# Ordering on VectorE around a deformable convolution: the combining step and the depthwise taps

## The chip, the core and the metric

The kernel runs on one core of a Trainium2 chip. The metric is device time in microseconds (us) of one execution; lower is better. TensorE is PE in the profile, VectorE is DVE, ScalarE is ACT, GpSimd is POOL, and SP only issues DMAs.

## What is computed

The input is 32 images of 96 channels, 56 x 56 pixels, in float32. Two layers follow each other.

Layer 0 is an inverted residual block: a 1x1 convolution from 96 to 576 channels with SiLU, a 3x3 depthwise convolution with SiLU, a squeeze-and-excite gate, and a 1x1 convolution back to 96 channels, added to the input.

```python
h = silu(bn(conv1x1(x, w1)))
h = silu(bn(depthwise3x3(h, w2)))
h = h * se_gate(mean(h))
x1 = x + bn(conv1x1(h, w3))
```

Layer 1 makes an attention map from a Fourier magnitude, and then mixes an ordinary 3x3 convolution with a deformable one, whose nine taps are sampled bilinearly at learned offsets:

```python
y = x1 * ca * sa
offset = conv3x3(aux(y), off_w)
gate = sigmoid(conv1x1(relu(conv3x3(aux(y), dg1_w)), dg2_w))
y_def = einsum(bilinear_samples(y, offset), def_w) + def_b
z = (1 - gate) * conv3x3(y, base_w) + gate * y_def
out = relu(batchnorm(z) + x1)
```

## The kernel before

**Tiling.** Layer 1 goes through an image in seven bands of 8 rows (`j` from 0 to 6), and each band in two halves (`h`) of 28 columns. The main loop runs over all 224 bands (32 images by 7). While it works on image b, two generators ("streams") are advanced step by step inside it: `second(b + 1)` (projection of layer 0, Fourier part, attention) and `first(b + 2)` (expansion and depthwise convolution of layer 0). The function `pump()` advances them in proportion to the slots passed, and also runs functions that were put into the list `later` with a due slot.

**Who sets the order.** The Python code traces the instructions in one order. A scheduler then orders each engine's queue: by trace order as priority, and by its own model of when an instruction's inputs are ready. SP's queue alone is kept in traced order. A queue, once built, is executed strictly in its order, and each instruction waits there for its semaphores. Some instructions are pinned (`keep_in_program_order`): the product of the column and row weights (L710) is one of them, so it comes behind what was traced ahead of it on DVE.

**What a half band does** (L1136 and the lines behind it). `sample_tiles` (L739) multiplies transposed blocks of y by the bilinear weights `wc`, in two groups of matmuls; ScalarE copies the samples to `v` (L743) and packs them (L750). `deform` (L758) multiplies `v` by the deformable weights into the PSUM tile `pd`. That call is put into `ends` and made in the next half band, behind the first group of `sample_tiles`. Then, in the same place, come the blocks for a coming half (L721, L725, L727) and the product `wc = wc * wr` on DVE (L710) for the next half band's samples. So DVE's product of weights is always traced behind `ends`.

**The pool of `pd`** has one buffer. Both halves of a band write to one `pd`; `combine` (L797 to L800) reads it on DVE in its first instruction, and the first product of the next band may start only when that first instruction has ended. Before the change `end_half` puts `join`, which calls `combine`, into `later`, due two slots on.

**The offsets.** `offsets` runs a joint 3x3 convolution (L615) for the band two ahead of the main loop, ScalarE takes two parts out of its PSUM bank (L635, L637), and DVE copies the offsets out in two copies, `at` (L664). The bank comes free behind these copies. GpSimd then sends `at` to memory (L672).

**The taps.** The depthwise convolution is done by DVE: for each of nine units per image one multiplication (L260) and eight multiply-adds over 128 x 1512 or 128 x 1568 elements (L262). The first two images use matmuls for three of the taps (L246, L258). When a unit is complete, ScalarE applies SiLU (L222).

**Others on DVE** that matter here: the sums over the spectrum `m_fe` and `m_fy` (L436, L437), which PE waits for in L440; the sums of squares (L379); the largest offset, `top` (L676).

Of the kernel before, what the change touches and what calls it, by code (L numbers as in the profile page):

```python
# [1 line left out]

# [8 lines left out]
ALU = mybir.AluOpType  # L11
# [5 lines left out]
C, H, W = 96, 56, 56  # L17
# [18 lines left out]
BW = NBW  # L36
TS = 4
NTX = W // TS
# [79 lines left out]
def bank(p):  # L118
    return p["mm"].tile([128, 512], FP, name="mm")
# [84 lines left out]
def hidden(tc, p, x, xn, h2d, pooled, defer):  # L204


    nc = tc.nc
    w = p["w0"]

    def rows_of(x, half):  # L210
        xt = p["xt"].tile([C, (HH + 1) * W], FP, name="xt")
        r0 = half * (HH - 1)
        nc.sync.dma_start(xt, x[:, r0 : r0 + HH + 1].rearrange("c h w -> c (h w)"))
        return xt

    xts = p.pop("xts", None) or [rows_of(x, 0), rows_of(x, 1)]
    for _ in expand(nc, p, xts, UNITS[0]):
        yield
    def finish(u, acc):
        ch = UNITS[u][0]  # L220
        flat = acc.rearrange("p h w -> p (h w)")
        tc.keep_in_program_order(nc.scalar.activation(  # L222
            flat, flat, AF.Silu, bias=w["sh2"][:, ch : ch + 1], scale=w["inv2"][:, ch : ch + 1], accum_out=pooled[:, u : u + 1]))
        nc.scalar.dma_start(h2d[u], flat)

    before = None
    for u, (ch, half) in enumerate(UNITS):
        h1 = p["h1"]
        more = expand(nc, p, xts, UNITS[u + 1]) if u + 1 < len(UNITS) else iter(())
        if xn is not None and u in (5, 8):  # L230

            p.setdefault("xts", []).append(rows_of(xn, int(u == 8)))
        acc = p["acch"].tile([128, HH, W], FP, name="acch")

        rows_of_tap = lambda dy: (int(half == 0 and dy == 0), HH - int(half == 1 and dy == 2))
        diag = p.get("diag")
        taps = [k for k in (4, 0, 1, 2, 3, 5, 6, 7, 8) if diag is None or k not in TPE]
        parts = []
        if diag is not None:
            for r0 in range(0, HH, ER):  # L240
                pt = bank(p)[:, :EW].rearrange("p (h w) -> p h w", h=ER)
                for i, k in enumerate(TPE):
                    dy, dx = divmod(k, 3)
                    lo, hi = rows_of_tap(dy)
                    lo, hi = max(r0, lo), min(r0 + ER, hi)
                    nc.tensor.matmul(pt[:, lo - r0 : hi - r0], diag[:, ch, i], h1[:, dy + lo : dy + hi, dx : dx + W],  # L246
                                     start=(i == 0), stop=(i == len(TPE) - 1))
                parts.append((slice(r0, r0 + ER), pt))
            next(more, None)
            yield  # L250
        for n, k in enumerate(taps):
            dy, dx = divmod(k, 3)
            lo, hi = rows_of_tap(dy)
            win = h1[:, dy + lo : dy + hi, dx : dx + W]
            wk = w["w2"][:, ch, k : k + 1]
            if n == 0:
                for rs, pt in parts:
                    nc.vector.scalar_tensor_tensor(acc[:, rs], win[:, rs], wk, pt, ALU.mult, ALU.add)  # L258
                if not parts:
                    nc.vector.tensor_scalar(acc, win, wk, None, ALU.mult)  # L260
            else:
                nc.vector.scalar_tensor_tensor(acc[:, lo:hi], win, wk, acc[:, lo:hi], ALU.mult, ALU.add)  # L262
            if n % 2:
                if n == 3 and before:
                    finish(u - 1, before)
                next(more, None)
                yield
        for _ in more:
            pass
        before = acc  # L270
    defer(lambda: finish(len(UNITS) - 1, before))


def sigmoid(nc, out, src, bias):
# [354 lines left out]
def joint_conv(nc, p, yp, j, hid):  # L629


    w = p["w"]
    pa = bank(p)
    conv3(nc, pa[:, :BW], w["joint"], yp, CJ, j)
    nc.scalar.activation(hid, pa[:DMID, :BW], AF.Relu, bias=w["dg1b"][:DMID])  # L635
    yb = p["yb"].tile([C, BW], FP, name="yb")
    nc.scalar.activation(yb[BC:], pa[OFF0 + QC :, :BW], AF.Identity, bias=w["cv"]("base_b")[BC:])  # L637
    yield yb, pa[OFF0 : OFF0 + NOFF, :BW]
    pb = bank(p)
    for k in range(NTAP):  # L640
        dy, dx = divmod(k, 3)
        r0 = j * RB + dy + PD - 1
        for i in range(2):
            nc.tensor.matmul(pb[i * BC : (i + 1) * BC, : BW // 2].rearrange("p (h w) -> p h w", h=RB // 2), w["base"][:, k],  # L644
                             yp[:C, r0 + i * RB // 2 : r0 + (i + 1) * RB // 2, dx + PD - 1 : dx + PD - 1 + W],
                             start=(k == 0), stop=(k == NTAP - 1))
    yield
    for i in range(2):
        nc.scalar.activation(yb[:BC, i * BW // 2 : (i + 1) * BW // 2], pb[i * BC : (i + 1) * BC, : BW // 2], AF.Identity,
                             bias=w["cv"]("base_b")[:BC])  # L650
    yield


def offsets(nc, p, yp, j, top, hid, ybs, hds, defer):

    w = p["w"]
    joint = joint_conv(nc, p, yp, j, hid)
    yb, pa = next(joint)  # L660
    ybs.append(yb)
    at = p["off"].tile([NOFF, NTX, 2, TP], FP, name="at")
    for s in range(2):
        nc.vector.tensor_copy(at[:, :, s].rearrange("o t (r c) -> o t r c", r=TS),  # L664
                              pa[:, s * BW // 2 : (s + 1) * BW // 2].rearrange("o (r t c) -> o t r c", r=TS, t=NTX))
    yield
    yield
    next(joint)
    yield
    od = p["dp"].tile([NTX, 2, NOFF, TP], FP, name="od")  # L670
    p["tc"].keep_in_program_order(
        nc.gpsimd.dma_start(od.rearrange("t s o p -> o (t s) p"), at.rearrange("o t s p -> o (t s) p")))  # L672
    next(joint)
    yield
    next(joint, None)
    nc.vector.tensor_reduce(top, at.rearrange("o t s p -> o (t s p)"), AX.X, ALU.max, apply_absolute_value=True)  # L676
    for _ in range(7):
        yield
    ht = p["ht"].tile([SB * NTX, 4, KP], FP, name="ht")
    src = od.rearrange("t s o p -> t (s o p)").unsqueeze(0).to_broadcast([SB, NTX, 4 * KP])  # L680
    nc.sync.dma_start(ht.rearrange("q n k -> q (n k)"), src)
    for _ in range(3):
        yield

    def hats():
        ho = p["ht"].tile([SB * NTX, 2, 2, KP], FP, name="ho")
        p["tc"].keep_in_program_order(nc.scalar.activation(
            ho.rearrange("q x s n -> q s x n"), ht.rearrange("q (s x) n -> q s x n", s=2), AF.Abs, bias=w["blk"]))
        nc.scalar.activation(ho, ho, AF.Relu, bias=w["one"], scale=-1.0)
        hd = p["dp"].tile([2, 2, SB, NTX, KP], FP, name="hd")  # L690
        nc.scalar.dma_start(hd.rearrange("x s i t n -> (i t) (x s) n"), ho.rearrange("q x s n -> q (x s) n"))
        hds.append(hd)

    defer(hats)
# [99 lines left out]
def combine(nc, p, j, pd, yb, gate, st):  # L794

    z = p["q2"].tile([C, BW], FP, name="z")
    nc.vector.scalar_tensor_tensor(z, pd[:C, :BW], p["w"]["cv"]("def_b"), yb, ALU.add, ALU.subtract)  # L797
    nc.vector.scalar_tensor_tensor(z, gate, 1.0, z, ALU.add, ALU.mult)
    nc.vector.scalar_tensor_tensor(z, z, 0.5, yb, ALU.mult, ALU.add)
    nc.vector.bn_stats(st[:, j], z)  # L800
    return z
# [152 lines left out]
def layers(tc, a, dp, x1d, zd, stats, far):  # L954
# [6 lines left out]
    nc = tc.nc  # L961
    B = x1d.shape[0]
    with ExitStack() as ctx:
        p = {"tc": tc, "dp": ctx.enter_context(tc.tile_pool(name="l1d", bufs=3, space=DRAM))}
# [25 lines left out]
        streams, later = [], []  # L990
        slot = 0
# [68 lines left out]
        def store(b, j, z):  # L1060
            nc.gpsimd.dma_start(zd[b][:, j * BW : (j + 1) * BW], z)

        def join(n, pd, gate, st):
            b, j = bands[n]
            z = combine(nc, p, j, pd, ybs[n], gate, st)
            later.append((slot + 7, lambda: store(b, j, z)))
            if j == NBD - 1:
                nc.vector.bn_aggr(stats[:, b], st)

        def end_half(n, h, v, gate, st):  # L1070
            if h == 0:
                pds[n] = p["pd"].tile([128, 512], FP, name="pd")
            deform(nc, p, pds[n], v, h)
            if h:
                pd = pds.pop(n)
                later.append((slot + 2, lambda: join(n, pd, gate, st)))

        ends, pds = [], {}

# [41 lines left out]
        for n, (b, j) in enumerate(bands):  # L1121
            if j == 0:
                st = p["st"].tile([C, NBD, 6], FP, name="st")
# [7 lines left out]
            for h in range(2):  # L1131
                v = p["vp"].tile([128, NTAP, NTH, 2, TP], FP, name="v")
                prepare(2 * n + h + READY + AHEAD)
                s = ready.pop(0)
# [17 lines left out]
                if h == 0:  # L1152
                    if n % 2 == 0:
                        gates.extend(gates_of(nc, p, hids[n // 2]))
                    gate = gates.pop(0)
# [361 lines left out]
```

## Time and profile before

| what | value |
|---|---|
| median of 3 runs | 9030.57 us (9027.98 to 9034.88) |
| the profiled execution: its time / the span of its instructions | 9059.03 us / 9057.2 us |
| mean granted TensorE clock | 0.939 |
| PE busy | 8175.3 us, 90% of the span |
| DVE busy | 7184.4 us, 79% |
| ACT busy | 5393.5 us, 60% |
| POOL busy | 2902.8 us, 32% |
| the 2250 plain taps, L262 on DVE | 4456.4 us, 1981 ns each |

How to read it: busy time is the time in which an engine has an instruction at work. A line `engine line <- releaser: us, times, longest` in the table of waits is idle time of the first engine that ended when the second one finished. In the timeline each row is one instruction, or several of one kind that follow each other: start, duration, engine, line, operation, `output<-inputs`, and in brackets the idle time before it and what ended it. Durations of one row overlap those of the next by some tens of ns; on PE by more, as matmuls are pipelined.

### The profile page before, as it was taken

To read this page: it belongs to the slowest core of one execution; us is meant where nothing else is said; L and a number is where in the kernel's file an instruction comes from. 1 tells how busy PE (TensorE), PEld (TensorE's weight loads), DVE (VectorE), ACT (ScalarE), POOL (GpSimd) and SP (SyncE) were. 2 spreads that over 40 slices of the span, in tenths; PEclk is the share of its full clock that TensorE was granted. 3 is DMA by queue.
4 is the path that set the end of the run, shared out by engine and by line. 5 is a ranking of instruction groups with operands and counts; after the bars stand their busy time and mean duration, and the time that the engine had idled before them with its cause. 6 is when DMAs were issued, how large, how long until landed. Compare 5 with 4: busy or idle time off the path is not lost. (4 is left out here: it accounts for less than half of the span.)

```text
span 9057.2 us, 137476 instructions
## 1 busy us (share of the span) xinstructions
PE 8175.3 (90%) x52406; PEld 5193.5 (57%) x52406; DVE 7184.4 (79%) x6629; ACT 5393.5 (60%) x10486; POOL 2902.8 (32%) x2800
## 2 busy tenths in 40 slices
PE   5889999999999999999999999999999999999960
PEld 3456565665656566565656656565665655566640
DVE  7688888888888888888888888888888888888333
ACT  2356665666666666666666666666666666666553
POOL 0233333333333333333333333333333333333210
PEclk9889999999999999999999999999999999999985
DMA  2356666666666666666666666666666666666669
GB/s 82 108 142 160 163 169 165 157 154 153 163 166 171 166 157 147 158 165 164 172 161 154 159 157 168 165 174 161 154 154 160 165 166 172 166 156 144 144 188 416
DMA packets 1068758, 1486.48 MB, mean 164 GB/s; under 512 B 590191, under 2 KB 839839, under 8 KB 1055807
## 3 DMA queue, kind: packets, MB, share of 16 engines
q1 hardware_dynamic: 858995, 985.20, 46.4%
q10 hardware_dynamic: 153803, 329.80, 10.2%
q0 software_dynamic: 55296, 162.60, 6.7%
q8 instruction: 420, 6.88, 0.4%
q14 instruction: 244, 1.99, 0.1%
HBM read 1064.29 MB, written 412.65 MB: 163 GB/s over the span
## 5 line engine op out<-in xcount | busy, mean ns | idle before, releaser
L262 DVE SCALAR_TENSOR_TENSOR acch<-hp,w,acch 128x1512 f32<-128x1512 f32 (+1 forms) x2250 | 4456.4, 1981 | 141.4 <-ACT hp L173 103.8
L615 PE MATMUL mm<-yp,c_jointW 104*128 104x448 f32 x4032 | 1679.6, 568 | 10.1 <-DMA yp<-fqd 10.1
L758 PE MATMUL pd<-v,c_def 128*96 128x224 f32 (+1 forms) x6272 | 1468.8, 382 | 142.7 <-DVE z L797 115.6
L721 POOL COPY ybl<-yp 96x448 f32<-96x448 f32 x896 | 1048.3, 1198 | 1204.9 <-PE mm L725 1204.8
L758 PEld LDWEIGHTS pd<-v,c_def 128*96 128x96 f32 (+1 forms) x6272 | 1062.2, 176 | 449.8 <-issue 116.9
L615 PEld LDWEIGHTS mm<-yp,c_jointW 104*128 104x128 f32 x4032 | 776.6, 196 | 784.2 <-issue 747.4
L743 ACT COPY v<-mm 96x288 f32<-96x288 f32 (+1 forms) x2688 | 1004.3, 441 | 156.0 <-PE mm L739 109.3
L169 PE MATMUL mm<-xt,w 96*128 96x392 f32 (+3 forms) x2688 | 1058.5, 527 | 35.3 <-DMA xt<-in_x 33.1
L739 PE MATMUL mm<-wc,yt 64*96 64x144 f32 x12544 | 1056.9, 300 | 20.8 <-DVE sq L379 6.7
L739 PEld LDWEIGHTS mm<-wc,yt 64*96 64x96 f32 x12544 | 834.2, 164 | 317.3 <-issue 199.1
L173 ACT ACTIVATE hp<-mm,sh,inv 128x392 f32<-128x392 f32 (+2 forms) x1216 | 810.7, 673 | 344.8 <-PE mm L169 290.5
L710 DVE TENSOR_TENSOR wc<-wc,wr 128x1008 f32<-128x1008 f32 x448 | 566.6, 1265 | 412.5 <-DMA wr<-hd 385.1
L644 PE MATMUL mm<-yp,c_base0W 96*64 96x224 f32 x8064 | 830.1, 358 | 5.7 <-ACT hp L173 5.7
L329 PE MATMUL mm<-hq,w3s 128*96 128x392 f32 x2048 | 749.7, 510 | 63.6 <-DMA hq<-h2d 62.2
L672 POOL DMA_DIRECT2D od<-at x224 | 186.7, 834 | 1908.3 <-DVE at L664 1292.6
L750 ACT COPY v<-v 32x448 f32<-32x448 f32 x1344 | 755.1, 562 | 29.7
L727 ACT COPY yt<-mm 128x384 f32<-128x384 f32 (+1 forms) x896 | 353.9, 439 | 700.7 <-PE mm L725 699.0
L644 PEld LDWEIGHTS mm<-yp,c_base0W 96*64 96x64 f32 x8064 | 555.2, 135 | 282.7 <-issue 61.0
L635 ACT ACTIVATE hid<-mm,c_dg1b 50x448 f32<-50x448 f32 x224 | 140.8, 628 | 868.4 <-PE mm L615 858.4
L476 POOL TENSOR_TENSOR o<-o,xc 96x392 f32<-96x392 f32 x256 | 376.2, 1470 | 806.2 <-ACT o L339 804.2
L222 ACT ACTIVATE acch<-acch,sh,inv 128x1568 f32<-128x1568 f32 x288 | 488.4, 1696 | 202.8 <-DVE acch L262 176.5
L329 PEld LDWEIGHTS mm<-hq,w3s 128*96 128x96 f32 x2048 | 323.0, 166 | 395.2 <-issue 367.5
(194 smaller groups left out, 9325.3 us busy)
## 6 DMA issues: line engine op xcount, KB each, us to landing
h2d<-acch ACTq DMA_DIRECT2D x288, 784.0 KB
wc<-hd SPq DMA_DIRECT2D x896, 252.0 KB
wr<-hd SPq DMA_DIRECT2D x448, 504.0 KB
hq<-h2d SPq DMA_DIRECT2D x128, 980.0 KB
hq<-h2d SPq DMA_DIRECT2D x128, 784.0 KB
hq<-x1d SPq DMA_DIRECT2D x768, 98.0 KB
ht<-od SPq DMA_DIRECT2D x224, 252.0 KB
hd<-ho ACTq DMA_DIRECT2D x224, 252.0 KB
```

Source lines behind the costliest of these rows:

```text
L169: nc.tensor.matmul(pt[p0 : p0 + w1.shape[1], : rows * W], w1, xts[hf][:, r0 * W : (r0 + rows) * W], start=True, stop=True)
L173: nc.scalar.activation(h1[lo:hi, row0 : row0 + rows, 1 : 1 + W], pt[lo:hi, : rows * W].rearrange("p (h w) -> p h w", h=rows), AF.Silu, bia ...
L262: nc.vector.scalar_tensor_tensor(acc[:, lo:hi], win, wk, acc[:, lo:hi], ALU.mult, ALU.add)
L329: nc.tensor.matmul(pts[half][:C, :EW], w3s[:, ch], hq, start=(i == 0), stop=False)
L615: nc.tensor.matmul(view, weights[:, k], yp[:channels, r0 : r0 + RB, dx + PD - 1 : dx + PD - 1 + W], start=(k == 0), stop=(k == NTAP - 1))
L644: nc.tensor.matmul(pb[i * BC : (i + 1) * BC, : BW // 2].rearrange("p (h w) -> p h w", h=RB // 2), w["base"][:, k], yp[:C, r0 + i * RB // 2 ...
L710: p["tc"].keep_in_program_order(nc.vector.tensor_tensor(wc, wc, wr, ALU.mult))
L721: nc.gpsimd.tensor_copy(yb[:, :, s], blocks)
L739: nc.tensor.matmul(pt[k][:C, (t - lo) * KP : (t - lo + 1) * KP], yt[ps, t], s[ps, t * KP : (t + 1) * KP], start=True, stop=True)
L743: nc.scalar.copy(v[:C, :, lo:hi, k].rearrange("c k t p -> c t k p"), pt[k][:C, : (hi - lo) * KP].rearrange("c (t k p) -> c t k p", t=hi - ...
L750: nc.scalar.copy(v[C:, 1 + 2 * i : 3 + 2 * i], v[i * QC : (i + 1) * QC, KA:])
L758: nc.tensor.matmul(out.rearrange("c q (t x) -> c t q x", x=TS), p["w"]["def"][ks, k], v[ks, k].rearrange("c t s (r x) -> c t (s r) x", r=T ...
```

## The change

Three edits, all of them about order. No instruction is added or removed, and no size changes.

1. `join`, and so `combine`, is called at once behind the second half's products, in place of two slots later.
2. The first instruction of `combine` and each of the two copies of the offsets is remembered in `p["urgent"]`.
3. Each tap traced on DVE afterwards (L258, L262; not the first multiplication, L260) gets an edge behind the instruction that `urgent` names at that time. The edge has no semaphore: it only tells the scheduler that the tap must stand behind it in DVE's queue.

```diff
             if n == 0:
-                for rs, pt in parts:
-                    nc.vector.scalar_tensor_tensor(acc[:, rs], win[:, rs], wk, pt, ALU.mult, ALU.add)
+                with behind(p):
+                    for rs, pt in parts:
+                        nc.vector.scalar_tensor_tensor(acc[:, rs], win[:, rs], wk, pt, ALU.mult, ALU.add)
                 if not parts:
                     nc.vector.tensor_scalar(acc, win, wk, None, ALU.mult)
             else:
-                nc.vector.scalar_tensor_tensor(acc[:, lo:hi], win, wk, acc[:, lo:hi], ALU.mult, ALU.add)
+                with behind(p):
+                    nc.vector.scalar_tensor_tensor(acc[:, lo:hi], win, wk, acc[:, lo:hi], ALU.mult, ALU.add)
...
+def behind(p):
+
+    return p["tc"].issue_after(p["urgent"]) if "urgent" in p else nullcontext()
...
     for s in range(2):
-        nc.vector.tensor_copy(at[:, :, s].rearrange("o t (r c) -> o t r c", r=TS),
-                              pa[:, s * BW // 2 : (s + 1) * BW // 2].rearrange("o (r t c) -> o t r c", r=TS, t=NTX))
+        p["urgent"] = nc.vector.tensor_copy(
+            at[:, :, s].rearrange("o t (r c) -> o t r c", r=TS),
+            pa[:, s * BW // 2 : (s + 1) * BW // 2].rearrange("o (r t c) -> o t r c", r=TS, t=NTX)).ins
...
-    nc.vector.scalar_tensor_tensor(z, pd[:C, :BW], p["w"]["cv"]("def_b"), yb, ALU.add, ALU.subtract)
+    p["urgent"] = nc.vector.scalar_tensor_tensor(z, pd[:C, :BW], p["w"]["cv"]("def_b"), yb, ALU.add, ALU.subtract).ins
...
             if h:
                 pd = pds.pop(n)
-                later.append((slot + 2, lambda: join(n, pd, gate, st)))
+                join(n, pd, gate, st)
```

## The prediction

> **What bounds the kernel.** I read the page's first part, then PE's waits over the whole span, then DVE's queue around the longest of them. A change within 0.2% (18 us) can't be told from none here.
>
> ```profile
> PE 8175.3 (90%) x52406; PEld 5193.5 (57%) x52406; DVE 7184.4 (79%) x6629; ACT 5393.5 (60%) x10486; POOL 2902.8 (32%) x2800
> ```
>
> PE is busy for 90% of the span, and 94 to 95% of each 1000 us between 2000 and 8000 us: it is the bound, and what can be gained is its idle time. The rows of the waits that this change can touch:
>
> ```profile
> PE pd L758 <- DVE z L797: 115.6, 26, 6.1
> PE acc L440 <- DVE m_fy L437: 72.8, 30, 5.6
> PE acc L440 <- DVE m_fe L437: 71.1, 31, 2.5
> PE mm L725 <- DVE at L664: 57.2, 28, 5.7
> ```
>
> They are some 30 times each: once per image, not once per band. So I looked for the band. The `pd` wait is in the last band (j=6):
>
> ```profile
> 4485.99 1.52 DVE L710 TENSOR_TENSOR wc<-wc,wr 128x1008 f32<-128x1008 f32 x1 [4.10 <-DMA wr<-hd]
> 4487.44 5.91 DVE L262 SCALAR_TENSOR_TENSOR acch<-hp,w,acch 128x1568 f32<-128x1568 f32 x3
> 4493.38 0.68 DVE L797 SCALAR_TENSOR_TENSOR z<-pd,c_cvec,yb 96x448 f32<-96x448 f32 x1
> ```
>
> ```profile
> 4494.21 1.03 PE L758 MATMUL pd<-v,c_def 96*96 96x224 f32 x2 [6.02 <-DVE z L797]
> ```
>
> The products ended at 4483.84; DVE had a weights product waiting for its DMA and three taps in front of z. The `at` and `m_fy` waits are both in j=3, where DVE reaches `at` some 10 us late, having a queue of taps:
>
> ```profile
> 4370.29 0.77 PE L725 MATMUL mm<-c_ident,ybl 96*128 96x96 f32 x7 [0.96 <-DVE at L664]
> ...
> 4374.95 0.38 PE L440 MATMUL acc<-c_RT,m_fy 128*29 128x112 f32 x2 [2.74 <-DVE m_fy L437]
> ```
>
> **What the change does to the queues.** All counts stay; I laid the two built orders beside each other. Below, 0 is the end of a band's last product (L758), z is L797, z2 and z3 are L798 and L799, bn is L800. Both orders repeat with the image. From z on, DVE's queue for j=2, j=3 and j=5 (j=1 has one tap less, j=4 has none, j=6 one more and the aggregate L1068):
>
> ```
> before, j=2:  at at wc top tap tap tap | z tap z2 wc z3 tap bn
> after,  j=2:  at at tap top tap        | z tap z2 tap z3 tap bn wc
> ```
>
> Three things moved. z has fewer taps in front. The first `wc` product stood in front of z, and now stands behind z, its taps and bn: it is traced behind `ends`, is pinned there, and `combine` is now inside `ends`. And on PE the next band's first products come 1 to 4.5 us of PE work sooner, ahead of the samples that need this `wc`.
>
> **Removed.** (1) j=6: the last joint matmul ends 11.7 us before 0 (mean over the images), ACT's two copies take about 2, so `at` can start at -9.7. Then 0.7 for `at at`, two taps of 1.9, top 0.6, a memset 0.1: DVE stands at z at -4.5 and waits for PE. All 115.6 us go. (2) j=3: between the z of j=2 and `at` there are 10 taps, one L260, two `wc`, two L602 in both orders. But z of j=2 comes at about 0, not 3.8, and a DMA wait of 3.0 inside no longer shows, so `at` is on time (-7.8): 57.2 go. Then 0.7, two taps and top 4.4, L436 1.65, L437 2.55: `m_fy` is there at 1.5, PE's L440 comes at about 2: 72.8 go. Sum: 245.6, or 8.2 us per image over the 30 images whose main loop has taps.
>
> **Added.** PE's first sample product that needs the moved `wc` must now wait for z's stretch. Its length is in the trace, as two bands have this very order before the change:
>
> ```profile
> 4375.88 0.68 DVE L797 SCALAR_TENSOR_TENSOR z<-pd,c_cvec,yb 96x448 f32<-96x448 f32 x1
> 4376.48 1.83 DVE L262 SCALAR_TENSOR_TENSOR acch<-hp,w,acch 128x1568 f32<-128x1568 f32 x1
> 4378.24 0.61 DVE L798 SCALAR_TENSOR_TENSOR z<-gate,z 96x448 f32<-96x448 f32 x1
> 4378.77 1.84 DVE L262 SCALAR_TENSOR_TENSOR acch<-hp,w,acch 128x1568 f32<-128x1568 f32 x1
> 4380.54 0.61 DVE L799 SCALAR_TENSOR_TENSOR z<-z,yb 96x448 f32<-96x448 f32 x1
> 4381.07 1.84 DVE L262 SCALAR_TENSOR_TENSOR acch<-hp,w,acch 128x1568 f32<-128x1568 f32 x1
> 4382.84 0.62 DVE L800 BATCH_NORM_STATS2 st<-z 96x6 f32<-96x448 f32 x1
> 4383.37 1.19 DVE L710 TENSOR_TENSOR wc<-wc,wr 128x1008 f32<-128x1008 f32 x1
> ```
>
> From z's start to wc's end: 8.68 us. z can't start before 0. A tap in it is worth 1.77, so j=1 has 7.3 (two small instructions come in) and j=6 10.7; j=4, without taps, 4.5 by the same instructions after z in that band before. j=3 adds a late z: `m_fy` at 1.5 and one L260 put z at 2.7, so wc ends at 11.4.
>
> Against that stands PE's own work between 0 and that sample product in the new order: each instruction at its line's mean start-to-start time without waits, times 0.95 (the old order worked out so gives 4.4 for j=2, the trace 4.3). Even and odd images differ a little.
>
> | band | PE needs wc at | wc ends | PE waits |
> |---|---|---|---|
> | j=0 | 22 | under 10 | 0 |
> | j=1 | 6.6 / 6.9 | 7.3 | 0.7 / 0.4 |
> | j=2 | 7.3 / 8.2 | 8.7 | 1.4 / 0.5 |
> | j=3 | 7.0 / 6.2 | 11.4 | 4.4 / 5.2 |
> | j=4 | 4.7 / 4.7 | 4.5 | 0 |
> | j=5 | 7.5 / 7.5 | 8.7 | 1.2 / 1.2 |
> | j=6 | 4.2 / 6.3 | 10.7 | 6.5 / 4.4 |
>
> Sum 14.2 and 11.7, mean 13.0 per image, times 30: **390 us**. Before the change the same `wc` was done 2 to 12 us ahead of need; PE's wait for it was 5.2 us in all.
>
> **Edits costed at nothing.** The sooner products need ScalarE's copies of `v` (2.6 in most bands) and packs (3.2 to 6.0): mostly there in time; where not (j=6, packs at 5.4), the wc wait behind it covers it. Bounds: 0, and 0.5 for each of 210 bands, 105 us, 0.5 being the mean of the 36 waits of PE for `v` (19.3 us). `m_fe` (j=0 to 1): DVE has two taps and one wc more in front, less 4.7 us of its own waits that they fill, less a z that starts 8 us sooner: it ends within 1 us of before; bounds -30 and +75 (1 to 2.5 us per image). GpSimd's sends of `at` and of z get their data sooner or at the same time. The weight loads (SP) need a `wr` buffer freed by the wc of one band earlier: they issue 13 us or more behind 0 in most bands, the wc now ends by 11.4; nothing. DVE has 16% idle in the steady part, about 41 us per image, so z's waits for PE (up to 5 us a band) can be afforded.
>
> **The clock.** After the 6.02 us gap TensorE ran at half clock:
>
> ```profile
> 4494.20:4502.90 8.70, 8.69 (x31) 6.41 (x32) 5.42 (x9) 1.27 (x3) 1.57 (x3) 0.50 0.94 199
> ```
>
> That costs some 4.3 us more per such gap. I leave it out on both sides, as j=6 keeps a gap as long and j=3 gets one of 4.4 to 5.2 for two shorter ones. The Trainium skill ("TensorE: Matmul & The Clock Gate", HAM oscillation) says that an idle gap of over about 3.4 us brings the half clock. By this rule the sum stays for j=6 and gets worse for j=3; removing the `pd` gap outright would have been worth its gap and half of the slow stretch.
>
> **Sum.** 390 - 245.6 = +144 us on 9057.2, so about 9200 in a profiled execution. Profiled time is 9059.03 against a median of 9030.57, 0.3% more; on the median the same +140 gives **9170**.
>
> **Rivals.**
> - *Faster: the wc product is in time.* Break-even is 8.2 us of waits per image against my 13.0. With four to five waiting bands that is 1 us per band: if z's stretch takes 7.7 and not 8.7, or PE's work in front is 1 us longer, it is a draw, and from there on the change wins. For it: the table's PE times are sums of means. Against: the stretch was measured, in two bands of each image pair. With 2.5 us per band off the waits (j=3 3, j=6 3, the rest 0) 6 per image are left, 180 in all, and the half clock behind j=6 goes too (3 us is short of the 6.02 that brought it; 30 x 4.3 = 130): 180 - 246 - 130 = -196, 8835.
> - *Much slower: DVE's waits spill over.* Taps now stand behind z and `at`. ScalarE's SiLU on a finished unit (L222) stands in its queue up to 3 us before the taps are done in j=1 and j=2 (4 to 5 us behind them before), and holds the copies of `v` up. Two such per image at 2.5: +150, 9320.
> - *The change doesn't act:* its effects fall within 0.2% either way. The built orders differ as said, so only by cancellation: 9030.
>
> **Chances.** Forecast (9050 to 9270) 0.62; much slower 0.18; cancelling 0.07; faster 0.13. Faster by over 0.2% 0.13, within 0.07, slower 0.80. The range goes from 9000 (z's stretch 1 us shorter, and `m_fe` at its better bound) to 9310 (the ScalarE bounds of 105 us and a little more); outside are most of the faster case and the end of the slower.
>
> **What would show it.** Right: PE's wait for z L797 and for `at` gone; a new row of PE's L739 waiting for DVE's wc product of some 300 to 400 us, in j=3 and j=6 above all; DVE waiting for `pd` longer than 166.1 us, as z now mostly waits for PE. Wrong: no such row, or `m_fy` still there at 70 us, or a new row of PE waiting for ScalarE.

## The result and the profile after

The changed kernel takes **9522.4 us** (9515.9 to 9550.4) beside 9032.7 us of the kernel before on the same chip: 1.0545 times as long, 95% interval 1.0521 to 1.0570. The forecast was 9170, range 9000 to 9310. The direction was right, the size was not: +140 was forecast and +490 measured. The profiled execution has a span of 9526.1 us and a mean granted clock of 0.918 (0.939 before).

Lines have moved, the taps by two and the rest by seven or eight: z is now L805, the copies of the offsets L671, `wc` L718, the samples L747, the products L766, the taps L264, `yp` L609. First the busy times on the page after:

```profile
PE 8372.5 (88%) x52406; PEld 5356.3 (56%) x52406; DVE 6965.1 (73%) x6629; ACT 5406.8 (57%) x10486; POOL 3172.7 (33%) x2800
```

PE has the same 52406 instructions and is busy 197 us longer. Up to its last matmul (9237.0 us, 8768.4 before) it is also idle 271 us longer, 864 in place of 593. These two make up the 468 us of this profile. PE's waits, after:

```profile
PE mm L747 <- issue: 360.1, 113, 6.9
PE pd L766 <- DVE z L805: 116.5, 34, 6.5
...
PE pd L766 <- ACT v L758: 55.6, 32, 2.7
...
PE acc L447 <- DVE m_fy L444: 30.1, 32, 4.4
```

The wait for `at` is gone. `m_fy` is down from 72.8 to 30.1, and a wait of the samples has come. "Issue" says that the profile shows no releaser for it; the timelines below show what it is. The wait for z has its old size, but in another place: 83 of the 116.5 us are in j=2 of the odd images and 21 in j=3 of the odd images. These are DVE and then PE behind the last product of j=2 in an odd image (the products ended at 4777.87):

```profile
4776.95 2.19 DVE L264 SCALAR_TENSOR_TENSOR acch<-hp,w,acch 128x1568 f32<-128x1568 f32 x1
4787.67 0.68 DVE L609 SCALAR_TENSOR_TENSOR yp<-yp,ca,sab 96x448 f32<-96x448 f32 x1 [8.53 <-DMA yp<-x1d]
4788.39 0.68 DVE L805 SCALAR_TENSOR_TENSOR z<-pd,c_cvec,yb 96x448 f32<-96x448 f32 x1
...
4795.82 1.19 DVE L718 TENSOR_TENSOR wc<-wc,wr 128x1008 f32<-128x1008 f32 x1
```

```profile
4782.16 1.00 PE L789 MATMUL mm<-hid,dg2p 50*96 50x448 f32 x4
4789.21 4.55 PE L766 MATMUL pd<-v,c_def 96*96 96x224 f32 x14 [6.05 <-DVE z L805]
4797.11 1.85 PE L747 MATMUL mm<-wc,yt 64*96 64x144 f32 x12 [3.35 <-issue]
```

DVE has nothing left to do at 4779.1, but `yp` stands in front of z and waits for its DMA for 8.53 us, and z behind it. The products wait 6.05 us for z. Then the samples wait 3.35 us: they start at 4797.11, and `wc` ends at 4795.82 + 1.19 = 4797.01. So "issue" is the wait for `wc`. Of the 416.5 us that PE idles in front of the sample matmuls, 404 end within 0.25 us behind the end of a `wc` product; before the change it was 11 of 20.8.

In the even image j=2 has the second wait alone:

```profile
5056.18 0.68 DVE L805 SCALAR_TENSOR_TENSOR z<-pd,c_cvec,yb 96x448 f32<-96x448 f32 x1 [2.50 <-PE pd L766]
5056.78 2.50 DVE L264 SCALAR_TENSOR_TENSOR acch<-hp,w,acch 128x1568 f32<-128x1568 f32 x1
5059.20 0.97 DVE L806 SCALAR_TENSOR_TENSOR z<-gate,z 96x448 f32<-96x448 f32 x1
...
5064.99 1.18 DVE L718 TENSOR_TENSOR wc<-wc,wr 128x1008 f32<-128x1008 f32 x1
```

```profile
5066.28 1.84 PE L747 MATMUL mm<-wc,yt 64*96 64x144 f32 x12 [3.07 <-issue]
```

z is on time here, and z's stretch up to the end of `wc` is 9.99 us long. What the 3.07 us brought with them is in the two windows that follow; columns: stretch, length, busy time of PE, PEld, DVE, ACT and POOL, granted clock, DMA share, GB/s.

```profile
5065.80:5072.50 6.70, 6.22 (x31) 5.06 (x31) 6.70 (x7) 2.56 (x5) 0.00 (x0) 0.50 0.71 174
5072.60:5079.00 6.40, 6.40 (x68) 4.55 (x68) 6.33 (x5) 5.93 (x13) 6.33 (x3) 1.00 0.03 8
```

For 6.7 us PE runs at half clock: 12 matmuls of the samples take 1.84 us, 1.07 in e8 at full clock, shown below. From start to start, samples in this trace take 127.5 ns each in half clock and 66.6 ns in full, and the other large groups of matmuls 1.9 to 2.1 times as long. Summed over the trace up to the last matmul, the half clock is granted for 823 us before and 1270 us after. PE is busy in it 702 and 1029 us. Half of those 327 us more, **164 us, is an estimate of the time lost to the clock** alone, most of the 197 us of added busy time.

### The profile page after: what moved, and what is told of

It is laid out like the page before. It is cut to its first block, busy times and chain, and to the rows that moved or that the text cites. A ratio compares the mean times of both kernels' runs of the same rounds, so it can differ in the third digit from the quotient of the medians.

```text
span 9526.1 us, 137514 instructions
## 1 busy us (share of the span) xinstructions
PE 8372.5 (88%) x52406; PEld 5356.3 (56%) x52406; DVE 6965.1 (73%) x6629; ACT 5406.8 (57%) x10486; POOL 3172.7 (33%) x2800
## 5 line engine op out<-in xcount | busy, mean ns | idle before, releaser
L264 DVE SCALAR_TENSOR_TENSOR acch<-hp,w,acch 128x1512 f32<-128x1512 f32 (+1 forms) x2250 | 4237.2, 1884 | 105.3 <-ACT hp L173 83.4
L729 POOL COPY ybl<-yp 96x448 f32<-96x448 f32 x896 | 1454.3, 1650 | 2363.9 <-PE mm L733 2358.9
L766 PE MATMUL pd<-v,c_def 128*96 128x224 f32 (+1 forms) x6272 | 1447.2, 380 | 178.7 <-DVE z L805 116.5
L747 PE MATMUL mm<-wc,yt 64*96 64x144 f32 x12544 | 1165.7, 317 | 416.5 <-issue 360.1
L766 PEld LDWEIGHTS pd<-v,c_def 128*96 128x96 f32 (+1 forms) x6272 | 1060.8, 175 | 510.5 <-issue 194.7
L747 PEld LDWEIGHTS mm<-wc,yt 64*96 64x96 f32 x12544 | 908.2, 175 | 716.4 <-issue 570.8
L169 PE MATMUL mm<-xt,w 96*128 96x392 f32 (+3 forms) x2688 | 1093.4, 541 | 34.3 <-DMA xt<-in_x 33.3
L336 PE MATMUL mm<-hq,w3s 128*96 128x392 f32 x2048 | 771.9, 522 | 8.6 <-DMA hq<-h2d 6.3
L718 DVE TENSOR_TENSOR wc<-wc,wr 128x1008 f32<-128x1008 f32 x448 | 573.5, 1285 | 242.0 <-DMA wr<-hd 230.3
L651 PEld LDWEIGHTS mm<-yp,c_base0W 96*64 96x64 f32 x8064 | 578.1, 135 | 237.8 <-issue 47.5
L671 DVE COPY at<-mm 18x224 f32<-18x224 f32 x448 | 154.6, 380 | 658.0 <-ACT yb L644 617.5
L805 DVE SCALAR_TENSOR_TENSOR z<-pd,c_cvec,yb 96x448 f32<-96x448 f32 x224 | 152.1, 679 | 597.0 <-PE pd L766 595.3
L169 PEld LDWEIGHTS mm<-xt,w 96*128 96x128 f32 (+1 forms) x2688 | 369.4, 181 | 330.2 <-issue 176.9
L483 POOL TENSOR_TENSOR o<-o,xc 96x392 f32<-96x392 f32 x256 | 322.2, 1259 | 647.8 <-ACT o L346 645.9
```

Source lines behind the costliest of these rows:

```text
L169: nc.tensor.matmul(pt[p0 : p0 + w1.shape[1], : rows * W], w1, xts[hf][:, r0 * W : (r0 + rows) * W], start=True, stop=True)
L336: nc.tensor.matmul(pts[half][:C, :EW], w3s[:, ch], hq, start=(i == 0), stop=False)
L718: p["tc"].keep_in_program_order(nc.vector.tensor_tensor(wc, wc, wr, ALU.mult))
L729: nc.gpsimd.tensor_copy(yb[:, :, s], blocks)
L747: nc.tensor.matmul(pt[k][:C, (t - lo) * KP : (t - lo + 1) * KP], yt[ps, t], s[ps, t * KP : (t + 1) * KP], start=True, stop=True)
L766: nc.tensor.matmul(out.rearrange("c q (t x) -> c t q x", x=TS), p["w"]["def"][ks, k], v[ks, k].rearrange("c t s (r x) -> c t (s r) x", r=T ...
```

## The experiments

Theory **W**: the added time is PE's wait for the moved `wc`, and the half clock that each such wait brings. Theory **D**: it is the edges, which push the taps back on DVE. The table has all kernels; the ratio is to the kernel before, measured beside it on the same chip (there it takes 9026 to 9048 us). "Samples idle" is PE's whole idle time in front of the sample matmuls, "at wc" the part of it that ends within 0.25 us behind the end of a `wc` product. "Idle" and "half clock" are PE's up to its last matmul. All are in us of the profiled execution. Times of one band, here and below, run from the end of its last product to the end of the next band's, as means over the images 4 to 29, even and odd apart.

| kernel | median us | ratio, interval | samples idle | at wc | idle | half clock |
|---|---|---|---|---|---|---|
| before | 9032.7 | 1 | 20.8 | 11 | 593 | 823 |
| changed | 9522.4 | 1.0545 (1.0521 to 1.0570) | 416.5 | 404 | 864 | 1270 |
| e1, wc first | 9195.9 | 1.0182 (1.0148 to 1.0216) | 135.4 | 12 | 671 | 881 |
| e2, no edges | 9740.2 | 1.0784 (1.0762 to 1.0805) | 520.9 | 516 | 920 | 1625 |
| e3, yp behind z | 9514.5 | 1.0538 (1.0513 to 1.0563) | 428.8 | 417 | 821 | 1263 |
| e4, 16 small matmuls | 9663.4 | 1.0707 (1.0681 to 1.0734) | 192.7 | 162 | 581 | 1120 |
| e5, wc before taps | 9519.3 | 1.0537 (1.0519 to 1.0554) | 321.4 | 311 | 832 | 1198 |
| e6, e1 and yp behind z | 9292.6 | 1.0285 (1.0267 to 1.0302) | 129.3 | 12 | 689 | 993 |
| e7, edges behind at | 8983.1 | 0.9941 (0.9923 to 0.9959) | 36.7 | 12 | 565 | 689 |
| e8, 7 small matmuls | 9400.4 | 1.0408 (1.0388 to 1.0427) | 273.4 | 264 | 685 | 1000 |
| e9, both edges alone | 8947.0 | 0.9906 (0.9885 to 0.9926) | 54.6 | 10 | 548 | 628 |
| e10, e7, early, wc first | 9078.8 | 1.0059 (1.0040 to 1.0079) | 108.0 | 11 | 582 | 795 |
| e11, e7, early | 9467.8 | 1.0493 (1.0474 to 1.0512) | 416.2 | 413 | 834 | 1215 |
| e12, e9, wc last | 9588.7 | 1.0594 (1.0563 to 1.0625) | 392.9 | 390 | 849 | 1464 |

**e1: wc traced first.**

```diff
+                        ready.extend(weights(nc, p, *ws) for ws in loads[:1])
+                        del loads[:1]
                         for end in ends:
                             end()
...
-                        ready.extend(weights(nc, p, *ws) for ws in loads[:1])
-                        del loads[:1]
```

> The changed kernel with the product of the weights (wc) traced ahead of the second half's products and of the combining step again, as it was before; the early combining and the edges of the taps stay. Theory W (the moved wc product is the cause, by PE's waits for it and by the half clock behind these waits): PE's wait for wc falls from about 400 us to under 60, the half clock to last matmul from 1270 us to 850 to 1000, DVE's wait for pd stays near 600 us, and the time comes to 8960 us (8880 to 9060), near the kernel before. Theory D (the edges are the cause: DVE idles 429 us longer for pd and does its taps later, and this spills over to PE): the wait of DVE for pd stays and so does the time, 9300 us or more.

Measured 9195.9: the place of `wc` is worth 326 us. W's waits and half clock went as it said (404 to 12 us at `wc`, 1270 to 881 us); its time did not, as 163 us above the kernel before stayed. DVE's wait for `pd`, which both theories had at some 600 us, fell to 260. j=6 is 5 to 7.5 us shorter than before the change, but two bands are longer. One is j=2 of the even image, by 9 us, as `yp` with its DMA wait stands in front of z. The other is j=0, by 5 us: PE's samples wait there, and not for `wc`, but for a sum of squares that DVE does behind a tap:

```profile
PE mm L747 <- DVE sq L386: 81.6, 30, 3.4
```

**e2: the early combining without edges.**

```diff
 def behind(p):
-    return p["tc"].issue_after(p["urgent"]) if "urgent" in p else nullcontext()
+    return nullcontext()
```

> The changed kernel without the edges of the taps: only the combining step is called at once, so wc still stands behind it. In the built queue z's stretch is short in two of the bands (a tap less), and two to four taps stand in front of z and of the copies of the offsets again. Theory W: PE waits for wc some 200 us (j=3 and j=6 above all), the waits for pd in j=6 and for the copies in j=3 are back, 250 us together; the time is 9310 us (9150 to 9450). Theory D: without the edges the loss is gone, 9030 us (8980 to 9080).

D is out as the cause of the loss: without edges the loss is larger, not gone (9740.2). W's mechanism is there (516 us of waits for `wc`, where some 200 were expected), but of the 250 us of waits for z and `at` that it expected back only 78 us came, for z, and both theories' sizes are wrong. The edges keep taps out of the way; which of the two kinds pays is seen in e11.

**e3: yp put behind z in the changed kernel.**

```diff
-                later.append((slot + 4, lambda args=args: attend_rows(nc, p, b, *args)))
+                later.append((slot + 12, lambda args=args: attend_rows(nc, p, b, *args)))
...
-    nc.vector.scalar_tensor_tensor(rows, rows, p["ca", b], sab, ALU.mult, ALU.mult)
+    with behind(p):
+        nc.vector.scalar_tensor_tensor(rows, rows, p["ca", b], sab, ALU.mult, ALU.mult)
```

> The changed kernel with the attention product on the rows of y (yp, which waits for a DMA) traced eight slots later and put behind z by the same kind of edge, so that it stands in front of no z any more; in the changed kernel it stands in front of z in j=1 to 2 of every second image. Theory W (with a part for yp): PE's wait for pd behind z falls from 116.5 us to under 40, half clock down by 100 us or more, the time 9385 us (9340 to 9450). Theory without a part for yp: the wait only changes its name, 9500 us (9470 to 9550).

The wait for z fell from 116.5 to 40.8 us, and the odd j=2 from 51.0 to 44.6 us, yet the time is the same (9514.5). The odd j=3 grew from 32.6 to 36.4 us, the even j=2 and j=3 by 2.1 and 2.2, and the half clock stayed (1263). The theory without a part for `yp` had it right: `yp` is not a term that can be taken out by itself. The wait was real, its removal paid nothing.

**e4 and e8: more work where PE waits.**

```diff
+                if h == 1 and (j - 1) % NBD in (2, 3, 5, 6):
+                    pds[n] = p["pd"].tile([128, 512], FP, name="pd")
+                    for _ in range(7):
+                        nc.tensor.matmul(pds[n][:C, BW:512], p["w"]["def"][:C, 0], p["w"]["def"][:C, 1, : 512 - BW],
+                                         start=True, stop=True)
```

This is e8; e4 has 16 for 7, and j=1 too. The tile of `pd` is then not allocated again for the products, so that the wait for z stands in front of the small matmuls (116.6 us in e8).

> The changed kernel with 16 small matmuls more (96x64, results never read) per band in the bands behind j=1, 2, 3, 5 and 6, on constants, into columns of pd that nobody reads, traced ahead of the samples that wait for wc: some 2.4 us of PE work per band, about 380 us in all at full clock, 310 us of them in places where PE waits. No wait is shortened for DVE. Clock theory (the waits cost their length and then the half clock behind them, 1270 us of it against 823): the half clock falls below 1000 us and the time falls although there is more work, to 9400 us (9300 to 9470). Rival (the clock has no part in it): the time is the same or longer by the matmuls that lie outside waits, 9520 to 9650 us.

Missed: 9663.4, slower. The small matmuls took 578.6 us, not 380, and j=1, where nothing waits, got its share. Still the other matmuls were busy 8229 us in place of 8372, 144 us less for the same work, and of that busy time 790 us in place of 1029 lay in half clock. This was the clock at work, and the dose was too large. So e8:

> The changed kernel with 7 small matmuls more (96x64, 0.28 us each as e4 showed, results never read) ahead of the samples that wait for wc, behind j=2, 3, 5 and 6 alone: 7.8 us per image, 250 us of added work in all, meant to lie in waits. Clock theory: idle time of PE falls by some 200 us, the other matmuls are busy some 110 us less as the half clock falls to about 1050 us, and the time falls to 9440 us (9380 to 9500) with more work. Rival (the clock has no part): 9520 to 9600 us.

Right, and a little more than that: **with 217 us of added work the kernel is 122 us faster** (9400.4). Idle time fell by 180 us, and the other matmuls were busy 8233 us in place of 8372, 140 us less. Of that, half clock explains all: 742 us of their time lie in it in place of 1029, and half of the difference is 143. The even j=2 band in e8, in PE's timeline and the window behind:

```profile
4999.94 1.33 PE L1147 MATMUL pd<-c_def 96*96 96x64 f32 x14
5001.10 2.84 PE L766 MATMUL pd<-v,c_def 96*96 96x224 f32 x14
5005.88 1.07 PE L747 MATMUL mm<-wc,yt 64*96 64x144 f32 x12 [1.93 <-issue]
```

```profile
5006.00:5012.70 6.70, 6.70 (x61) 5.60 (x62) 6.70 (x6) 5.50 (x13) 2.57 (x2) 1.00 0.62 169
```

The gap is 1.93 in place of 3.07 us, the clock behind it stays at 1.00, and the 12 sample matmuls take 1.07 in place of 1.84 us.

**e5: taps behind wc, not behind z.**

```diff
-    p["tc"].keep_in_program_order(nc.vector.tensor_tensor(wc, wc, wr, ALU.mult))
+    p["urgent"] = nc.vector.tensor_tensor(wc, wc, wr, ALU.mult)
+    p["tc"].keep_in_program_order(p["urgent"])
+    p["urgent"] = p["urgent"].ins
```

(and `yp` as in e3)

> The changed kernel with the combining still called at once, but with every tap given its edge behind the moved wc product too, so that no tap stands between z and wc any more (z, z2, z3, bn, wc: 4.5 us where it was 8.5 to 10), and with yp behind wc by the same kind of edge, since it would else stand there with its DMA wait. Theory W, in its form with the stretch (the price of the moved wc is the length of what stands between z and wc): PE's wait for wc falls from 360 us to 100 or less, what is left of it in j=0 and j=3; the wait for pd is under 40 us; the half clock falls from 1270 us to about 900; 9050 us (8960 to 9180). Theory D (what costs is that taps come late): the taps come later still, 9350 us or more.

W missed: 9519.3, no change; D's forecast of 9350 or more was met. In j=2 it did what it should: 42.8 to 38.4 us (even) and 51.0 to 41.8 (odd). But j=6 got worse, with waits of 6.7 and 5.6 us for `wc` where there were 4.0 and 3.2. DVE and PE behind an even j=6:

```profile
4683.45 0.86 DVE L810 SCALAR_TENSOR_TENSOR z<-z,yb 96x448 f32<-96x448 f32 x1
4687.68 0.91 DVE L386 TENSOR_REDUCE sq<-hq 112x56 f32<-112x448 f32 x1 [3.37 <-DMA hq<-x1d]
...
4689.42 1.14 DVE L719 TENSOR_TENSOR wc<-wc,wr 128x1008 f32<-128x1008 f32 x1
```

```profile
4690.66 1.85 PE L750 MATMUL mm<-wc,yt 64*96 64x144 f32 x12 [5.67 <-issue]
```

The place that the taps left was given to a sum of squares that waits for a DMA. An edge says what must not stand there, and nothing of what the scheduler puts there instead. j=1 of the even image is 5 us longer too, with 12.6 us of half clock. Whether later taps cost something as well, as D has it, was not followed; PE's wait for layer 0's rows (L336) rose from 6.3 to 84.3 us, which would fit.

**e6: e1 with yp behind z**, the diffs of e1 and e3 together.

> The kernel of e1 (wc ahead of the second half's products again) with yp put behind z by an edge, eight slots later. In e1 the band j=2 of every second image was 9 us longer, as yp stood in front of z there with its DMA wait; the band j=0 was 5 us longer, as wc stands behind the copies of the offsets there. Theory yp (that yp in front of z is what e1 had left of the loss, with j=0): j=2 goes back by 9 us in half of the images, 145 us: 9050 us (9000 to 9130). Rival, after e3 (what yp gives in one band is lost in the next): 9150 to 9220 us.

The even j=2 fell from 45.2 to 37.4 us as the first theory had it, but the even j=4 rose from 35.7 to 45.6, and the time to 9292.6, above both theories' ranges. In that j=4 PE waits 3.8 us for ScalarE's copy of `v` ahead of the blocks (L734); that this copy is late through the DMA wait of `yp` was not followed.

**e7: edges behind the copies of the offsets alone.**

```diff
-    p["urgent"] = nc.vector.scalar_tensor_tensor(z, pd[:C, :BW], ...).ins
+    nc.vector.scalar_tensor_tensor(z, pd[:C, :BW], ...)
...
-                join(n, pd, gate, st)
+                later.append((slot + 2, lambda: join(n, pd, gate, st)))
```

> The kernel before with edges of the taps behind the two copies of the offsets alone: the combining stays two slots later, z names no edge. In the built queue two taps stand behind the copies in j=3 that stood in front of them, wc stays in front of z. Theory W (the edges are worth what they remove): PE's waits for at (57.2 us) and for m_fy (72.8 us) are gone, the wait for pd in j=6 stays near 116 us, no wait for wc: 8940 us (8860 to 9040) with the half clock of j=3 gone too. Theory D (edges push the taps back, and DVE ends later): 9100 us or more.

**e9: both edges, no early combining**, the second line pair of e7's diff alone.

> The changed kernel with its edges (behind z and behind the copies of the offsets) and without the early combining, which stays two slots later: the second and third edit without the first. Its built queue on VectorE is that of e1. If the three parts add up (edges behind at: -48 us as in e7; edges behind z: the rest up to e1; early combining: only through wc's place): 9196 us (9150 to 9240). If calling the combining early has a cost or gain of its own, the time differs from e1 by more than 45 us.

Both are faster than the kernel before, e7 by 0.59% (0.41 to 0.77) and **e9 by 0.94% (0.74 to 1.15), the best kernel of this study**. D had it the wrong way round for this case: with the combining two slots later the edges are a gain. But e7's time lies in W's range by luck. Of its waits only those for `at` and `wc` went as expected. `m_fy` stayed, and the wait for z fell from 115.6 us although z names no edge:

```profile
PE acc L447 <- DVE m_fy L444: 68.0, 31, 3.3
...
PE pd L766 <- DVE z L805: 43.2, 44, 1.8
```

The expectation of e9 was wrong in its first part. Its queue is not that of e1, for which I had taken it: `wc` stands in front of z in the same six bands, but in e9 two more taps follow it there in j=1, 2, 5 and 6, and `yp` stands in front of z in j=0 and not in j=2. And e1 and e9 differ by 249 us, so that the early combining with its other order costs something even where `wc` goes first: 123 us of PE's idle time and 125 us of busy time, as 792 us of it in place of 565 lie in half clock. DVE and PE in an even j=2 of e9, products ending at 4796.55:

```profile
4796.45 2.14 DVE L718 TENSOR_TENSOR wc<-wc,wr 128x1008 f32<-128x1008 f32 x1
4798.51 4.78 DVE L264 SCALAR_TENSOR_TENSOR acch<-hp,w,acch 128x1568 f32<-128x1568 f32 x2
4803.33 0.68 DVE L805 SCALAR_TENSOR_TENSOR z<-pd,c_cvec,yb 96x448 f32<-96x448 f32 x1
```

```profile
4800.85 0.98 PE L747 MATMUL mm<-wc,yt 64*96 64x144 f32 x12
...
4804.06 2.89 PE L766 MATMUL pd<-v,c_def 96*96 96x224 f32 x14 [0.50 <-DVE z L805]
```

z comes 6.8 us after the products and costs PE 0.50 us. PE has the samples first and the next band's products behind them, so it has 7.0 us of work before it asks for z. In the changed kernel it is the other way round: products 4.2 us, samples 10.1 us behind the last product (mean of the even j=2). It is the place of `wc` that turns PE's order, not the early combining. Where `wc` is traced first, whether the combining is early (e1, e6, e10) or not (before, e7, e9), the 12 sample matmuls that need it stand ahead of the next band's first product in every j from 1 to 6. Where it stands behind the combining (changed, e2, e3, e8, e11, and e12 with the combining two slots later), they stand behind that product in j=1, 2 and 3. In e5, where no tap delays `wc`, they stand ahead of it again in j=1 and 2. So the late `wc` also makes z urgent, which it had not been.

**e10 and e11: e7 with the combining called early**, `wc` traced ahead of it (e10) or behind it (e11).

> e7 (edges behind the copies of the offsets alone) with the combining called at once, but with wc traced ahead of it. If only wc's place makes the early combining dear: the time of e7, 8983 us (8940 to 9030). If the early combining costs by itself: 9080 us or more.

> e10 with wc traced behind the combining, as in the changed kernel; z names no edge. Theory W: PE waits for wc 200 to 350 us and the half clock grows by 200 us or more over e10's; from e1 to the changed kernel the same move cost 326 us, here one to two taps fewer stand in z's stretch: 9230 us (9130 to 9380). Theory D (without z's edges the taps are not late and nothing is lost): 8990 us.

From e7 to e10: +96 us, from e10 to e11: +389. Here, too, the early combining costs something by itself, and four times as much through `wc`. In e11 the half clock went as W said; the wait for `wc` (413 us) and the time (240 us more) lie above its ranges. These kernels also show what z's edges are worth. With the combining two slots later they gain 36 us (e7 to e9; the two intervals just touch). With it early they cost 117 us (e10 to e1) and 55 us (e11 to the changed kernel), and there the edges behind `at` are the gain: 272 us from e2 to e11. So D has a part for z's edges, though a small one.

**e12: e9 with wc traced behind the deferred combining.**

```diff
+                        if h == 0 and n:
+                            later.append((slot + 2, lambda: ready.extend(weights(nc, p, *loads.pop(0)) for _ in loads[:1])))
+                        else:
                             ready.extend(weights(nc, p, *ws) for ws in loads[:1])
                             del loads[:1]
```

> e9 (both kinds of edges, the combining two slots later) with one thing moved: the first wc product of a band is traced right behind the deferred combining, no longer behind the products alone. So z comes when it comes in e9, and wc stands behind it. Theory W (wc's place is dear by itself, as from e1 to the changed kernel, +326 us, and from e10 to e11, +389 us): PE waits for wc 250 to 400 us, the half clock goes from 628 us to about 1050, 9300 us (9180 to 9420). Rival (it is the early z, with the products of the next band coming early, that makes wc late): 9050 us or less.

The rival is out: `wc`'s place alone, with the combining called two slots later, costs 642 us (8947.0 to 9588.7; 621 by the two ratios), twice what W said. PE is idle 301 us longer, with 390 us of waits for `wc` in place of 10, and busy 342 us longer: 8459 us against 8117. The clock accounts for the second part, as 1289 us of the busy time lie in half clock in place of 565. In PE's order the products come first again (4.2 us behind the last product in the even j=2, the samples at 11.2): the scheduler puts the samples back when their `wc` comes late. What else that does is seen in j=1, where no gap is long:

```profile
4801.35 0.30 PE L550 MATMUL acc<-thT,fe 29*56 29x56 f32 x2 [0.39 <-ACT t L552]
4801.49 0.26 PE L551 MATMUL acc<-thM,fe 29*56 29x56 f32 x2
4802.15 0.31 PE L557 MATMUL acc<-twT,t 56*56 56x56 f32 x2 [0.39 <-ACT t L552]
4804.02 0.43 PE L557 MATMUL acc<-twT,t 56*56 56x56 f32 x2 [1.57 <-ACT s L558]
```

```profile
4803.30:4820.00 16.70, 15.98 (x67) 10.02 (x68) 11.26 (x10) 9.62 (x23) 1.39 (x2) 0.50 0.55 135
```

A chain of small matmuls, each waiting for ScalarE, is interleaved with the products in e9, where it has none of these gaps. With the products in front in one block it stands alone, with gaps of 0.39 to 1.57 us, and 17 us of half clock follow: j=1 takes 39.7 and 42.1 us, 33.8 and 32.3 in e9.

## Why the prediction was wrong

By its own steps:

- **The added wait for wc: right**, its mechanism and PE's turned order too. 390 us forecast, 416.5 - 20.8 = 396 measured, at the sample matmuls as described. The size is partly luck, by balance: j=3 was over-estimated (4.4 and 5.2 against 3.6 and 2.2), j=2 and j=5 under-estimated (1.4 and 0.5 against 3.1; 1.2 against 2.5 and 2.4). In j=6 the 6.5 and 4.4 forecast are 4.0 and 3.2 for `wc` and, ahead of them, 2.2 and 1.3 for ScalarE's packs, which the forecast had taken to be covered. z's stretch of 8.68 us was taken from j=3; in the even j=2 shown above it is 9.99, with a tap of 2.50 and an L806 of 0.97 us in place of 1.83 and 0.61.
- **"All 115.6 us go": the second step that failed.** They went from j=6, and 116.5 us came elsewhere, 83 of them in j=2 of the odd images. The prediction's queue of j=2 has no `yp` in front of z, as the odd images have, and so nothing of its DMA wait of 8.53 us. e3 showed that this term can't be had back singly: without it the time is the same.
- **`at` 57.2: right.** **`m_fy` 72.8: 43 of it** went.
- **ScalarE's packs, costed at nothing: 55.6 us** in place of 3.3, inside the bounds that I gave (0 to 105); the copies of `v` went from 19.3 to 3.0. Against it, a wait for layer 0's rows (62.2 us, L329) shrank to 6.3, which I had not listed.
- **"I leave the clock out on both sides": this is the step that failed by most.** It was argued from the two longest gaps, j=6 and j=3, and there it held. But the new waits of 2 to 3 us in j=2 and j=5 bring the half clock as well: it went from 0 to 7.9 and 14.2 us per j=2 band (even and odd), from 0.8 and 1.3 to 3.4 and 3.7 per j=5. In all 164 us; about half of it is in the odd j=2, where the 6.05 us wait for z is one of the gaps, so that this half goes with the term above. e8 took 140 us of busy time out by shortening gaps. The Trainium skill ("TensorE: Matmul & The Clock Gate", HAM oscillation), which I weighed, has the half clock behind gaps of over about 3.4 us; the changed kernel's trace has it in or behind 74 of the 82 gaps of 2.0 to 3.0 us (between 1000 and 8600 us), and the measurement decides. The same page (Part 1) speaks of a free-running window of 4096 cycles; that agrees with the 3.41 us grid described below.

The sum with what was measured: 396 of wc, -57 of `at`, -43 of `m_fy`, and about 0 of z, is 296 us; packs, layer 0's rows and small rows bring PE's idle time to +271; then 164 of the clock and 33 us of busy time that I can't place: 468 in the profile, where 144 had been forecast. Neither miss alone explains the result: with the 164 us added, or the 117 us for z, the forecast would still be far below what was measured.

The rivals: the wc product was not in time. Taps behind z did not spill over through ScalarE's SiLU: its wait for a last tap fell from 176.5 us to 32.5. DVE waits 595 us for `pd` (166.1 before), as forecast; that this costs nothing is not shown, as e9, which is faster, has 83.7 us of it. What would have corrected the forecast was in the trace of before: `m_fe`'s gaps of 2.4 us in j=0 stood beside 4.7 to 6.0 us of half clock per band there.

**What stays open.** On one path the parts add up: -79 us for the edges (e9, beside the kernel before on its chip), +249 for the early combining with `wc` first (e1), +326 for `wc`'s move, 496 in all. But they depend on their order: the same move costs 642 without the early combining. Each edit gives another order on all engines, and the 249 us were traced to bands (7.7 us in the even j=2, with `yp` in front of z; 1 to 2 us in j=0, j=1 and j=5), not to a cause each. That PE's turned order is what makes a late z and a late `wc` dear is read from the timelines; it was not tried by fixing PE's order alone. Why the moved `wc` costs 326 us on one path and 642 on another is open too.

## What to carry to other kernels

Before an instruction is made early, look at who asks for it and when, and at what is pinned behind it: here nobody asked for z until the samples were done, and making it early put the weights behind it. With the weights late, PE's order turned round, and z became urgent. Price a new wait of the bounding engine at its length plus half of the slow stretch that follows it, and count waits of 2 us as well as those of 6. An edge that keeps bulk work behind the few instructions that others wait for was a gain by itself here, and in part a loss beside the early combining; try it alone, and read what the scheduler puts in the freed place.

## What the runs showed of the hardware

- In every trace of this study half-clock stretches of TensorE begin on a fixed grid of 3413.3 ns (the phases of all stretches of a trace agree to within 1% of a period), and last a whole number of periods, but for the last one, with which the trace ends: in the changed kernel 68 of one, 83 of two, 32 of three, and few longer, of 192.
- Over the twelve traces without added matmuls (all but e4 and e8), between 1000 and 8600 us, the share of PE's gaps with a half-clock stretch that begins in them or within one period behind: 23% for 0.5 to 1.0 us, 47% for 1.0 to 1.5, 59% for 1.5 to 2.0, 79% for 2.0 to 3.0, 84% for 3.0 to 3.5, and 98% above. That the short ones count where several lie in one period is read from e12's j=1, not tested. Why a stretch lasts one period or five was not settled.
- In all fourteen traces PE's busy time with the program's own matmuls, less half of its part in half clock, lies between 7814 and 7886 us, though that busy time itself goes from 8117 to 8497 us. So nearly all of the difference in busy time between these kernels is the clock's.
- Filling part of the gaps with matmuls that nobody reads lowered the half clock from 1270 to 1000 us and made the kernel 122 us faster (e8); more than twice as many made it 141 us slower (e4).
